# Attention weights turned by VectorE blocks and DMA in place of TensorE, one four-bank score tile, and a stepwise preparation of tokens, in a four-layer transformer kernel

## The chip, the cores and the metric

The program runs on one core of one Trainium2 chip. The metric is the device time in microseconds (us) of one execution. The time before is 2130.87 us, the median of three runs (2130.27 to 2134.04).

## The reference, cut to what matters

The input x has 8 batches of 256 tokens and 512 features, in float32, and stays float32 throughout. Four layers follow one another. Layers 0, 1 and 2 hold an attention, layers 0 and 1 also an MLP, and layer 3 holds eight small experts. The part that the change touches is the attention over one sequence of 256 tokens:

```python
q, k, v = ...                       # layer 0: 8 heads of 64 (one k, one v); layer 1: 16 heads of 32
scores = q @ k.T (+ bias)           # per batch and head: 256 x 256
attn = softmax(scores)
ctx = attn @ v                      # per head: 256 x head size
x = x + ctx_of_all_heads @ Wo.T     # layers 0 and 2; layer 1 adds a bias and multiplies by gamma1
```

Layer 1 divides q and k by their norms per head and has an additive bias of 256 x 256. Layer 2 has a fixed sparse mask. The MLPs go from 512 to 2048 features and back.

## The kernel before, in words

All engines work from one program whose order within each engine is fixed when it is built. A tile scheduler merges the emitted steps into one queue for each engine and places the semaphore waits. Tiles come from pools by tag: a pool "A" of four PSUM banks, a pool "C" of four PSUM banks, a pool "p" of seven SBUF buffers of 512 columns, and so on (`BUFS`, L41). A new tile waits until everything that read the oldest tile of its tag is done.

`attend` (from L611) runs an attention. Its loop has one iteration for each batch b (8) and group g of four heads: two groups in attention0 (layer 0), four in attention1 (layer 1) and attention2 (layer 2). An iteration works on two groups at once:

1. `scored` computes the scores of the new group, four heads in four separate one-bank A tiles (matmul L645), queries on the partitions.
2. `turned` turns the softmax weights of heads 0 and 1 of the group before: four TensorE transposes for each head, against an identity, into a C bank (L702), and one copy back to p, on VectorE (L460) for even heads and on ScalarE (L464) for odd ones.
3. `softmax` of the new group: VectorE takes the row maximum (L659, attention0), or adds the bias and takes the minimum of the negative in one custom operation for each 128 x 256 half (L667, attention1 and 2); ScalarE takes the exponential with a row sum (L672). Reciprocals of the sums (L678) are transposed on VectorE (L682), written to DRAM by a DMA, `spread` (L685), and read back broadcast over partitions by one or two DMAs (L690).
4. `some(quantum)` emits a share of queued work: the projections of the next batch, matmul L585, and the output projection of the batch before.
5. `turned` for heads 2 and 3, then `weighted` (matmul L717, weights times values), then `divided` (VectorE L732 multiplies by the broadcast reciprocals and writes ctxT).
6. after the last group of a batch, its output projection is queued (matmul L585 `C<-wo,ctxT`).

In attention1 and attention2, `prepare` (L500 on) also normalizes the tokens two batches ahead (VectorE L450), transposes them on VectorE in 32 x 32 blocks (L515), writes the tile to DRAM in four DMAs of 128 KB that permute the blocks (`turn`, L520), and `fetch` reads it back (L533, L539), so that tokens become feature-major without TensorE. A scale and a shift then follow on VectorE L472 and ScalarE.

All these DMAs are issued by SyncE (SP), one queue in program order: a wait of one DMA holds those behind it. `project1` prepares q and k of attention1: VectorE adds the bias (L1367), ScalarE squares (L1369), VectorE sums (L1370), GpSimd takes the power -1/2 of 32 columns at once (L1379) and multiplies q and k by it (L1383), TensorE transposes them (L1355).

The MLPs (`mlp`) accumulate four products in the four A banks (L955), which `combined` reads out once for each batch and half (L966 to L974), and compute their up products in C (L908).

Of the kernel before, what the change touches and what calls it, by code (L numbers as in the profile page):

```python
# [32 lines left out]
P = 128  # L34
B, S, D = 8, 256, 512
NT = B * S // P
TB = S // P
# [4 lines left out]
    "n": 4, "hT": 2, "qT": 2, "kT": 2, "v": 2, "ctxT": 6, "p": 7, "qk": 4, "row": 3, "wbig": 8,  # L42
    "A": 4, "C": 4,
# [45 lines left out]
PI_BELOW = 3.1415925  # L89

# [21 lines left out]
def layout(inputs):  # L112
# [10 lines left out]
    def grouped(w):  # L123
# [20 lines left out]
        "bias": np.ascontiguousarray(a["mask_1x1xSxS_ff0"].reshape(S, S)),  # L144
        "vec": np.ascontiguousarray(np.concatenate([vec[k] for k in VEC], 1)),
# [26 lines left out]
class Program:  # L172
# [22 lines left out]
    def bank(self, tag):  # L195
        return self.t([P, 512], tag)

# [25 lines left out]
    def setup(self):  # L223
# [40 lines left out]
        self.n_turn = 0  # L264
        self.half_pi = c([P, 1], "half_pi")
# [156 lines left out]
    def normed(self, xs, eps, rms=False, outs=None):  # L422


        nc = self.nc
        n = len(xs)
        mv = self.t([P, n, 2], f"mv{n}", 2)
        r = self.t([P, n], f"r{n}", 2)
        for i, x in enumerate(xs):
            st = self.t([P, 6], "st", 3)  # L430
            nc.vector.bn_stats(st, x)
            nc.vector.bn_aggr(mv[:, i, :], st)  # L432
        mean, var = mv[:, :, 0], mv[:, :, 1]
        if rms:
            nc.vector.tensor_tensor(r, mean, mean, ALU.mult)
            nc.vector.tensor_tensor(r, r, var, ALU.add)
            nc.gpsimd.tensor_scalar(r, r, eps, None, ALU.add)
        else:
            nc.gpsimd.tensor_scalar(r, var, eps, None, ALU.add)  # L439
        nc.gpsimd.tensor_tensor(r, r, self.neg_half[:, 0:n], ALU.pow)  # L440
        rows = []
        for i, x in enumerate(xs):
            if outs is None:
                y = self.bank("n")
            else:
                y, x = outs[i], x.rearrange("p (k c i) -> p c k i", k=KC, c=4)
            if rms:
                nc.vector.tensor_scalar(y, x, r[:, i : i + 1], None, ALU.mult)
            else:
                nc.vector.tensor_scalar(  # L450
                    y, x, mv[:, i, 0:1], r[:, i : i + 1], ALU.subtract, ALU.mult
                )
            rows.append(y)
        return rows

    def copy(self, i, out, in_, scale=None):

        if i % 2 == 0:
            if scale is None:
                self.nc.vector.tensor_copy(out, in_)  # L460
            else:
                self.nc.vector.tensor_scalar(out, in_, scale, None, ALU.mult)
        elif scale is None:
            self.nc.scalar.copy(out, in_)  # L464
        else:
            self.nc.scalar.activation(out, in_, AF.Copy, scale=scale)

    def modulated(self, i, out, in_, scale, shift):
        if shift is None:
            self.copy(i, out, in_, scale)  # L470
        elif i % 2 == 0:
            self.nc.vector.tensor_scalar(out, in_, scale, shift, ALU.mult, ALU.add)  # L472
        else:
            self.nc.scalar.activation(out, in_, AF.Identity, bias=shift, scale=scale)
# [27 lines left out]
    def prepare(self, name, b, quick=False):  # L502
# [5 lines left out]
        hT = self.t([P, KC * S], "hT")  # L508
        if quick:
            self.ready[name, b] = [hT, self.normed(xs, eps, rms), None, 0]  # L510
            return
        nc = self.nc
        y = hT.rearrange("p (c k t i) -> p c k t i", c=4, k=KC, t=TB)
        self.normed(xs, eps, rms, [y[:, :, :, t, :] for t in range(TB)])
        nc.vector.transpose(hT, hT)  # L515
        kept = self.turns[self.n_turn % 3]
        self.n_turn += 1
        to = kept.rearrange("(c i) (a x) -> a i c x", c=4, a=4)
        for a in range(4):
            nc.sync.dma_start(  # L520
                to[a], hT[32 * a : 32 * a + 32, :].rearrange("p (c x) -> p c x", c=4)
            )
        self.ready[name, b] = [hT, None, kept, 0]
# [17 lines left out]
    def h(self, name, b, quick=False):  # L541


        if (name, b) not in self.ready:
            self.prepare(name, b, quick)
# [12 lines left out]
        def placed(i, c, in_):  # L558
            scale = mod[:, scale_at + c, b : b + 1]
            shift = None if shift_at is None else mod[:, shift_at + c, b : b + 1]  # L560
            self.modulated(i, place[:, c], in_, scale, shift)

        if rows is None:
            for c in range(KC):
                placed(c, c, place[:, c])
# [43 lines left out]
    def attend(self, name, n_groups, hd, project, value, finish, work, key_tiles=(2, 2), biased=None,  # L609
# [27 lines left out]
        def scored(b, g):  # L637
            lhs_rhs = [got[b][0](g, j) for j in range(4)]
            s = [self.bank("A") for _ in range(4)]
            rows = P // hd  # L640
            for j0 in range(0, 4, rows):
                for q in range(TB):
                    for j in range(j0, j0 + rows):
                        lhsT, rhs = lhs_rhs[j]
                        nc.tensor.matmul(  # L645
                            s[j][:, at[q] : at[q] + wide[q]], lhsT(q), rhs(wide[q]),
# [4 lines left out]
        def softmax(s):  # L651
            tot = self.t([P, 4, TB], "tot", 3)
            lows = self.t([P, 4, TB], "low", 3)
            ps = []
            for j in range(4):
                p = self.bank("p")[:, :total]
# [5 lines left out]
                for q in range(TB):  # L662
                    cols = slice(at[q], at[q] + wide[q])
                    src, sign = s[j], 1.0
                    if biased is not None:

                        nc.vector.tensor_tensor_reduce(  # L667
                            p[:, cols], s[j][:, cols], biased[:, cols], -1.0, BIG, ALU.add,
                            ALU.min, low[:, q : q + 1],
                        )  # L670
                        src, sign = p, -1.0
                    nc.scalar.activation(  # L672
                        p[:, cols], src[:, cols], AF.Exp, bias=low[:, q : q + 1], scale=sign,
                        accum_out=tot[:, j, q : q + 1],
                    )
                ps.append(p)
# [18 lines left out]
            return ps, by  # L695

        def turned(j, p):
# [9 lines left out]
            self.copy(j, p, m[:, :total])  # L707

        def weighted(b, g, pT):
            o = self.bank("C")  # L710
            for c in range(nch):
                for k in range(TB):
                    mine = [n for n, (kk, q) in enumerate(pairs) if kk == k]
                    q0 = pairs[mine[0]][1]
                    for i in range(per):
                        j = c * per + i
                        nc.tensor.matmul(  # L717
                            o[i * hd : (i + 1) * hd, c * S + q0 * P : (c + 1) * S],
                            value(got[b][1], g, j, k),
                            pT[j][:, mine[0] * P : (mine[-1] + 1) * P],  # L720
# [3 lines left out]
                        )  # L724
            return o
# [13 lines left out]
        last = None  # L739
        for i in range(B * n_groups + 1):  # L740
# [17 lines left out]
            if last is not None:  # L758
                for j in range(2):
                    turned(j, last[2][0][j])  # L760
            if ahead is not None:
                ahead = (b, g, softmax(ahead[2]))
                if g == 0 and ahead_of:
                    for c in (1, 2) if b == 0 else (b + 2,):
                        if c < B:
                            self.prepare(name, c, quick=c == 1)
                        elif c == B and after is not None:
                            self.prepare(after, 0)
                elif g == 0 and b == B - 1:
                    self.prepare(after, 0)  # L770
            if last is None:
                self.some(3 * quantum)
            elif ahead is None and then is not None:

                b, g, (pT, by) = last
                for j in range(2, 4):
                    turned(j, pT[j])
# [10 lines left out]
            else:  # L788
                self.some(quantum)
                b, g, (pT, by) = last  # L790
                for j in range(2, 4):
                    turned(j, pT[j])
# [58 lines left out]
    def blocked(self, b, hT):  # L851

        if b > 0:
            ts = [self.t([P, S], "ctxT") for _ in range(3)]
        else:

            ts = [t[:, i * S : (i + 1) * S] for t in (self.bank("qk"), self.bank("qk")) for i in range(2)]
            ts = ts[:3]
# [6 lines left out]
        return blocks  # L865

# [8 lines left out]
    def blocked_again(self, b):  # L875
# [3 lines left out]
        ts = [self.t([P, S], "ctxT") for _ in range(3)]  # L879
# [12 lines left out]
    def mlp(self, ups, downs, down_sums, load_ups, load_down, act, h, finish, tail):  # L892
# [29 lines left out]
        def sums(m):  # L922

            g = self.t([P, 4, P], "p")
# [4 lines left out]
            return g  # L929
# [15 lines left out]
        def lower(s, a, sums_of_a):  # L945
            hh, b, p = where(s)
            (y11, t3, y21, y22), (t1, t2, t4) = downs[4 * hh + p][:2]
            if p == 0:
                acc[:] = [self.bank("A") for _ in range(4)]
# [49 lines left out]
        for s in range(n):  # L999
            hh, b, p = where(s)  # L1000
            w = ups[4 * hh + p]
            if p == 0:
# [4 lines left out]
                else:  # L1007
                    ms = [begun(i, x) for i in w]
                    gs = [sums(m) for m in ms]
# [10 lines left out]
            if s > 0:  # L1020
                ms = [begun(i, x) for i in w]
                gs = [sums(m) for m in ms]
# [213 lines left out]
    def layer0_mlp(self):  # L1236
# [52 lines left out]
        def finish(hh, b, ys):  # L1289
# [7 lines left out]
            (self.project1(0, self.got), 22.1),  # L1297
# [36 lines left out]
    def project1(self, b, got):  # L1334
# [28 lines left out]
        for t in range(TB):  # L1363
            ss = self.t([P, 32], "ss", 2)
            q = yield from part(t, 0)
            qs = self.bank("qk")
            nc.vector.tensor_tensor(qs, q, self.q_bias, ALU.add)  # L1367
            sq = self.bank("n")
            nc.scalar.activation(sq, qs, AF.Square)  # L1369
            nc.vector.tensor_reduce(ss[:, 0:16], heads(sq), AX.X, ALU.add)  # L1370
            k_ = yield from part(t, 1)
            ks = self.bank("qk")
            nc.scalar.copy(ks, k_)
            sq = self.bank("n")
            nc.scalar.activation(sq, ks, AF.Square)
            nc.vector.tensor_reduce(ss[:, 16:32], heads(sq), AX.X, ALU.add)

            nc.gpsimd.tensor_scalar(ss, ss, 1e-24, None, ALU.max)
            nc.gpsimd.tensor_tensor(ss, ss, self.neg_half, ALU.pow)  # L1379
            nc.gpsimd.tensor_tensor(ss[:, 0:16], ss[:, 0:16], self.sm, ALU.mult)  # L1380
            for y, at in ((qs, 0), (ks, 16)):
                by = ss[:, at : at + 16].unsqueeze(2).to_broadcast([P, 16, 32])
                nc.gpsimd.tensor_tensor(heads(y), heads(y), by, ALU.mult)  # L1383
            ready.append((qs, ks))
# [26 lines left out]
    def layer1_attention(self):  # L1411
# [3 lines left out]
        self.ups, self.downs = [], []  # L1415

        for i in (0, 1, 2, -1, 3, -2, -3, -4):
            if i >= 0:
                self.layer1_up(i)
            else:  # L1420
                self.layer1_down(-1 - i)
# [22 lines left out]
        def value(v, g, j, k):  # L1444
# [3 lines left out]
            "attention1", 4, 32, self.project1, value, finish, (22.1, 6.8), biased=self.bias,  # L1448
# [8 lines left out]

    def layer1_up(self, i):
        self.ups.append([self.up_load("wfc1T", i)])

    def layer1_down(self, i):
# [3 lines left out]
            ([w[:, c, :] for c in range(4)], [w[:, c, :] for c in range(4, 7)], w[:, 7, :])  # L1465
        )

    def layer1_mlp(self):
# [5 lines left out]
        def act(i, ms, gs):  # L1474
            (m,), (g,) = ms, gs
# [6 lines left out]
            def later():  # L1482
                s = self.t([P, 4, P], "p")
# [78 lines left out]

    def layer2(self):
# [5 lines left out]
            biased=self.mask, extra={7: (self.expert_inputs(0), 1.74)},  # L1569
# [34 lines left out]
    def layer3(self):  # L1604
        nc = self.nc
        n_tiles = 4
        b1, b2 = self.v("b1"), self.v("b2")
# [6 lines left out]
        def hidden(xT, k):  # L1614

            got = [[], []]
            for f in range(2):
                ms = [self.bank("A") for _ in range(2)]
                for j in range(2):
# [4 lines left out]
                    )  # L1624
                for j in range(2):
                    e = 2 * k + j
                    g = self.bank("p")
# [124 lines left out]
```

## Time and profile before

| | before |
|---|---|
| median of three runs | 2130.87 us |
| profiled execution: time | 2125.73 us |
| profiled execution: span | 2123.8 us |
| mean granted TensorE clock | 0.994 |
| DMA moved | 138.18 MB |
| GpSimd busy | 291.3 us (14% of the span) |

The profile is of one execution. The page first gives the busy time of each engine: PE is TensorE's matmuls, PEld its weight loads, DVE VectorE, ACT ScalarE, POOL GpSimd. It then gives the chain of work that ended last, followed back from the last instruction, as shares of the span. After this come the groups of instructions: a line of the kernel, engine, operation, output tile and input tiles, count; busy time, mean duration; and the idle time of the engine before them with what ended it. The mean duration of a matmul is its latency through a pipeline; what matmuls cost in a row is read from pieces of the chain or from the timeline.

The execution falls into stages: attention0 from 50 to 300 us, mlp0 to 885, attention1 to 1295, mlp1 to 1675, attention2 to 1970, and layer 3.

### The profile page before, as it was taken

Reading aid. Unit: us, or ns where it says so; the run is one execution under the profiler, and the core shown is the slowest. Engines: PE = TensorE matmul, PEld = TensorE weight load, DVE = VectorE, ACT = ScalarE, POOL = GpSimd, SP = SyncE. Lnnn points to the kernel's source line nnn. Section 1 sums busy time; section 2 is a strip of 40 time slices with the busy share of each in tenths; the row PEclk is TensorE's granted clock in tenths of the full one; section 3 lists DMA queues with packets and bytes.
Section 4 is the critical chain, followed back from the end, with each engine's and each line's share of the span. In section 5 each row is a group of like instructions: output and inputs, shape, how many; then the busy total and the mean of one; then the engine's idle time right before and its main releaser. Section 6 shows DMA issues by size and latency. Waiting matters only on the chain.

```text
span 2123.8 us, 36492 instructions
## 1 busy us (share of the span) xinstructions
PE 2060.5 (97%) x13282; PEld 1523.8 (72%) x13282; DVE 1349.5 (64%) x4474; ACT 761.1 (36%) x2330; POOL 291.3 (14%) x308
## 2 busy tenths in 40 slices
PE   7999899999999999999999999999999989999999
PEld 4555569999999999855555547999999855555444
DVE  6856665656676555756666665776666777776333
ACT  3424321111111111245555663222222256566644
POOL 1101100000000000144444432000000101010220
PEclk9999999999999999999999999999999999999999
DMA  8320241211230100411112132233211222210001
GB/s 308 115 59 17 91 149 38 73 41 58 76 94 19 36 19 18 100 46 40 37 40 52 44 95 78 85 102 115 94 49 46 76 47 45 57 39 19 11 35 40
DMA packets 172147, 138.18 MB, mean 65 GB/s; under 512 B 77824, under 2 KB 144064, under 8 KB 171968
## 3 DMA queue, kind: packets, MB, share of 16 engines
q1 hardware_dynamic: 171968, 135.86, 21.6%
q8 instruction: 105, 1.72, 0.3%
q14 instruction: 74, 0.61, 0.1%
HBM read 99.87 MB, written 35.95 MB: 64 GB/s over the span
## 4 chain that ended last, share of the span: by engine, by line
PE 81%; DVE 8%; DMA 5%; ACT 2%; POOL 2%; issue 1%; SPq 1%; DVEq 0%; ACTq 0%; POOLq 0%
PE C L908 28%; PE C L585 20%; PE A L955 18%; PE C L702 4%; PE A L645 4%; PE C L717 3%; DMA wqkv<-spread 2%; DVE p L667 1%; PE A L1621 1%; DMA spread<-invT 1%; ACT p L672 1%; PE C L1639 1%; DMA turn<-hT 1%; DMA hT<-turn 1%; DVE p L460 1%
## 5 line engine op out<-in xcount | busy, mean ns | idle before, releaser
L908 PE MATMUL C<-hT,wbig 128*128 128x128 f32 x3072 | 416.3, 275 | 0.0
L908 PEld LDWEIGHTS C<-hT,wbig 128*128 128x128 f32 x3072 | 388.8, 192 | 8.6 <-issue 1.8
L585 PE MATMUL C<-wqkv,hT 128*128 128x512 f32 (+1 forms) x768 | 311.1, 545 | 4.9 <-DVE p L460 3.9
L908 PE MATMUL C<-ctxT,wbig 128*128 128x128 f32 x2160 | 300.0, 275 | 0.0
L672 ACT ACTIVATE p<-p,low 128x256 f32<-128x256 f32 (+1 forms) x512 | 241.9, 475 | 152.7 <-DVE low L667 152.0
L908 PEld LDWEIGHTS C<-ctxT,wbig 128*128 128x128 f32 x2160 | 270.1, 192 | 0.0
L955 PE MATMUL A<-wbig,p 128*128 128x256 f32 x1024 | 242.5, 379 | 0.0
L585 PEld LDWEIGHTS C<-wqkv,hT 128*128 128x128 f32 x768 | 130.9, 191 | 124.7 <-issue 111.2
L667 DVE CUSTOM_DVE_ANT_0 p<-A,row 128x256 f32<-128x256 f32 (+1 forms) x512 | 171.7, 386 | 70.6 <-PE C L717 55.1
L955 PEld LDWEIGHTS A<-wbig,p 128*128 128x128 f32 x1024 | 189.6, 190 | 23.0
L702 PEld LDWEIGHTS C<-ident,p 128*128 128x128 f32 x1152 | 129.3, 142 | 81.3 <-issue 39.6
L925 ACT COPY p<-C 128x128 f32<-128x128 f32 x192 | 51.3, 267 | 371.6 <-PE C L908 370.9
L936 DVE TENSOR_TENSOR p<-p,C 128x256 f32<-128x256 f32 x192 | 79.3, 421 | 162.7 <-PE C L908 160.8
L702 PE MATMUL C<-ident,p 128*128 128x128 f32 x1152 | 165.2, 282 | 15.2 <-DVE p L460 6.8
L585 PE MATMUL C<-wo,ctxT 128*128 128x512 f32 x336 | 158.7, 604 | 5.6 <-DVE ctxT L732 5.5
L439 POOL TENSOR_SCALAR r<-mv 128x2 f32<-128x2 f32 (+1 forms) x28 | 7.2, 256 | 953.0 <-DVE mv L432 953.0
L1276 ACT ACTIVATE p<-C 128x128 f32<-128x128 f32 x64 | 17.8, 278 | 295.9 <-DVE p L936 295.9
L926 DVE TENSOR_TENSOR p<-p,C 128x128 f32<-128x128 f32 x192 | 54.9, 286 | 101.5 <-ACT p L925 99.4
L460 DVE COPY p<-C 128x512 f32<-128x512 f32 (+1 forms) x160 | 100.7, 630 | 23.8 <-PE C L702 23.4
L585 PEld LDWEIGHTS C<-wo,ctxT 128*128 128x128 f32 x336 | 58.7, 190 | 70.5 <-issue 53.8
L672 ACT ACTIVATE p<-A,low 128x256 f32<-128x256 f32 x128 | 59.3, 478 | 120.5 <-DVE low L659 87.9
L464 ACT COPY p<-C 128x512 f32<-128x512 f32 (+1 forms) x160 | 85.5, 535 | 36.0 <-PE C L702 36.0
(226 smaller groups left out, 3064.7 us busy)
## 6 DMA issues: line engine op xcount, KB each, us to landing
turn<-hT SPq DMA_DIRECT2D x120, 128.0 KB
hT<-turn SPq DMA_DIRECT2D x16, 512.0 KB
kept<-hT SPq DMA_DIRECT2D x16, 512.0 KB
hT<-kept SPq DMA_DIRECT2D x16, 512.0 KB
wbig<-spread SPq DMA_DIRECT2D x64, 128.0 KB
hT<-turn SPq DMA_DIRECT2D x112, 64.0 KB
wbig<-in_wada1T SPq DMA_DIRECT2D x6, 1024.0 KB
ctxT<-kept SPq DMA_DIRECT2D x48, 128.0 KB
```

Of the source, the lines that this page charges most:

```text
L460: self.nc.vector.tensor_copy(out, in_)
L464: self.nc.scalar.copy(out, in_)
L585: self.nc.tensor.matmul(out, lhsT(k), rhs(k), start=(k == 0), stop=(k == n - 1))
L645: nc.tensor.matmul(s[j][:, at[q] : at[q] + wide[q]], lhsT(q), rhs(wide[q]), start=True, stop=True,)
L667: nc.vector.tensor_tensor_reduce(p[:, cols], s[j][:, cols], biased[:, cols], -1.0, BIG, ALU.add, ALU.min, low[:, q : q + 1],)
L672: nc.scalar.activation(p[:, cols], src[:, cols], AF.Exp, bias=low[:, q : q + 1], scale=sign, accum_out=tot[:, j, q : q + 1],)
L702: nc.tensor.transpose(m[:, n * P : (n + 1) * P], p[:, at[q] + k * P : at[q] + (k + 1) * P], self.ident,)
L717: nc.tensor.matmul(o[i * hd : (i + 1) * hd, c * S + q0 * P : (c + 1) * S], value(got[b][1], g, j, k), pT[j][:, mine[0] * P : (mine[-1] + 1 ...
L908: nc.tensor.matmul(m[:, c : c + P], w[:, k * P : (k + 1) * P], b[:, k], start=(first and k == 0), stop=(k == steps - 1), skip_group_check= ...
L926: nc.vector.tensor_tensor(g[:, 0, :], g[:, 0, :], m[:, P : 2 * P], ALU.add)
L936: nc.vector.tensor_tensor(g[:, 1:3, :], g[:, 0, :].unsqueeze(1).to_broadcast([P, 2, P]), m[:, 2 * P : 4 * P].rearrange("p (i t) -> p i t", ...
L955: nc.tensor.matmul(acc[at][:, half * S : (half + 1) * S], left, right, start=(p == 0 and half == 0), stop=(p == 3), skip_group_check=True,)
```

## The change: what it does

- In attention0 and attention1, batches 0 to 6, heads 0 and 1 of each group (`in_blocks` returns 2) are no longer turned by TensorE. Their keys are taken in another order by the score matmul (runs of 32 keys, strided), the exponentials are written to one two-bank tile in blocks, VectorE transposes that tile in 32 x 32 blocks, four DMAs write it to DRAM (`put`, the same pattern as for the tokens), and one DMA reads it back into the same tile. `weighted` reads it strided. Heads 2 and 3, attention2 and the last batch keep the TensorE path.
- A group's scores lie in one A tile of four banks, of which there is one (`"A": 1`); mlp and layer 3 use the same tile.
- The p pool has four two-bank buffers in place of seven one-bank ones, ctxT four buffers in place of six; the MLP's working tiles are regrouped to match, and `three` takes its extra blocks in turn from qk and ctxT.
- `prepare` is a generator: in attention1 and 2 it is emitted in up to three steps, one for each iteration, in place of all at once.
- The scale and shift of the fetched tokens (`placed`), and the matmuls that read turned weights, are kept in program order (`keep_in_program_order`), so the scheduler doesn't move other instructions of their engine past them.
- `project1` handles q and k separately (GpSimd power on 16 columns each, L1379 before), squares k straight from PSUM, and the start of layer 1 loads a copy of the bias in block order.

The diff, cut to its core:

```diff
-    "n": 4, "hT": 2, "qT": 2, "kT": 2, "v": 2, "ctxT": 6, "p": 7, "qk": 4, "row": 3, "wbig": 8,
-    "A": 4, "C": 4,
+    "n": 4, "hT": 2, "qT": 2, "kT": 2, "v": 2, "ctxT": 4, "p": 4, "qk": 4, "row": 3, "wbig": 8,
+    "A": 1, "C": 4,
...
+    def four(self):
+        t = self.t([P, 4, 512], "A")
+        return [t[:, i, :] for i in range(4)]
...
+    def in_blocks(self, name, b):
+        return 2 if name != "attention2" and b < B - 1 else 0
+
+    def put(self, kept, tile):
         to = kept.rearrange("(c i) (a x) -> a i c x", c=4, a=4)
         for a in range(4):
-            nc.sync.dma_start(
-                to[a], hT[32 * a : 32 * a + 32, :].rearrange("p (c x) -> p c x", c=4)
+            self.nc.sync.dma_start(
+                to[a], tile[32 * a : 32 * a + 32, :].rearrange("p (c x) -> p c x", c=4)
             )
...
         if rows is None:
             for c in range(KC):
-                placed(c, c, place[:, c])
+                self.tc.keep_in_program_order(placed(c, c, place[:, c]))
...
-            s = [self.bank("A") for _ in range(4)]
+            s = self.four()
...
+                        keys = rhs(wide[q])
+                        if j < self.in_blocks(name, b):
+                            keys = keys.rearrange("p (k c i) -> p c k i", c=4, i=32)
...
+                if j == 3 and n_blocks:
+                    nc.vector.transpose(blocks, blocks)
+                    kept = self.flips[self.n_flip % 4][:, : 2 * total]
+                    self.n_flip += 1
+                    self.put(kept, blocks)
+                    nc.sync.dma_start(blocks, kept)
             inv = self.inv[self.n_spread % 2]
...
-                for j in range(2):
-                    turned(j, last[2][0][j])
+                weights = last[2][0][1]
+                for j, p in enumerate(weights[: len(weights) // 2]):
+                    turned(j + len(weights) % 4 // 2, p)
...
-                            self.prepare(name, c, quick=c == 1)
+                            steps.append(self.prepare(name, c, quick=c == 1))
...
+                for step in steps:
+                    for _ in step:
+                        if b > 0 and ahead_of:
+                            break
+                    else:
+                        done.append(step)
...
-            nc.gpsimd.tensor_tensor(ss, ss, self.neg_half, ALU.pow)
...
+                nc.gpsimd.tensor_tensor(r, r, self.neg_half[:, 0:16], ALU.pow)
```

In the built program, the plain heads 2 and 3 are transposed in two places of an iteration (head 2 after the scores, head 3 later). The instruction queues of the two programs, which can be compared before any run, are used in the prediction.

## The prediction, on record before the run

> **What bounds the kernel now.** I read the page's busy times and chain first, then the busy times by stage, then the chain inside one batch of each attention. The page:
>
> ```profile
> PE 2060.5 (97%) x13282; PEld 1523.8 (72%) x13282; DVE 1349.5 (64%) x4474; ACT 761.1 (36%) x2330; POOL 291.3 (14%) x308
> ...
> PE 81%; DVE 8%; DMA 5%; ACT 2%; POOL 2%; issue 1%; SPq 1%; DVEq 0%; ACTq 0%; POOLq 0%
> ...
> L702 PE MATMUL C<-ident,p 128*128 128x128 f32 x1152 | 165.2, 282 | 15.2 <-DVE p L460 6.8
> ```
>
> TensorE is busy 97% of the span, so the whole program has 63 us without it. The 1152 turns at L702 are real TensorE work. By stage (columns: window, its length, PE, PEld, DVE, ACT, POOL busy, clock, DMA share, GB/s):
>
> ```profile
> 50.00:300.00 250.00, 233.04 (x1362) 139.50 (x1361) 166.17 (x464) 89.92 (x298) 35.13 (x61) 0.99 0.25 76
> 300.00:885.00 585.00, 585.00 (x4404) 560.29 (x4403) 367.21 (x1194) 91.40 (x281) 6.53 (x14) 1.00 0.18 55
> 885.00:1295.00 410.00, 397.50 (x2260) 214.50 (x2259) 259.77 (x879) 222.73 (x679) 172.01 (x126) 0.99 0.21 54
> ```
>
> The MLP has no gap at all. Attention0 has 17 us of gaps and attention1 12.5 us. So TensorE work removed from an attention counts in full, unless it turns into a wait there. What ends last inside a batch decides that. In attention0 the chain from 179 to 212 us has:
>
> ```profile
> 199.60 1.97 DMA spread<-invT
> ...
> 202.18 8.14 DMA wqkv<-spread
> 210.32 0.02 issue
> 210.34 0.44 DVE ctxT L732
> 210.78 0.04 issue
> 210.82 1.55 PE C L585 x3
> ```
>
> This batch runs from 179.49 to 210.82, 31.3 us with 29.9 of PE; its end is a DMA, the broadcast of the reciprocals. In attention1 a batch lasts 47.6 us (1113.65 to 1161.28) with 46.5 of PE: PE sets it.
>
> **Removed work.** Two heads of four transposes go in 2 × 7 groups of attention0 and 4 × 7 of attention1, 42 groups × 8 = 336 turns. The row's 282 ns is latency; in the chain eight in a row take 0.87 to 1.02 us ("1106.06 0.87 PE C L702 x8", "1112.63 1.02"), so one takes 0.116. That is 0.93 a group, 39 us in all: 13 in attention0 (1.86 a batch), 26 in attention1 (3.7 a batch). Per group one VectorE copy (0.63, L460) and one ScalarE copy (0.54, L464) go too, and one VectorE block transpose comes (1.2, the 128x1024 L515). VectorE gains 0.6 us a group; it is under 65% busy in both attentions, so I cost it at nothing unless it sits ahead of a copy that PE awaits, then 0.6.
>
> **Strided operands.** No row shows these. By the nearest row they are free: L908's hT operand is already read in 32-element runs, and twelve 128-column pieces take 1.50 us in the timeline (1424.15), less a latency of 0.275 0.111 each, while L585's dense 512-column ones take 7.03 for sixteen (1161.12), 0.107 for 128 columns. Taking that 4% on the 16 affected matmuls a group (about 2 us) as the upper end gives 0.08 a group, 3 us in all; the lower end is zero[...]. I take zero.
>
> **The DMA turn.** Four puts and one get are the same pattern as the tokens' L520 and L533/L539. The trace's chain shows 3.08 us from the last issue to landing (1067.42, 1251.96), issues of 0.3 to 0.6 each, and 3.94 and 4.61 us for gets. A flip lasts 1.2 + 1.8 + 3.1 + 4 ≈ 10 us. The Trainium skill speaks against it: "VectorE: DVE Perf Modes", section "The three transpose paths", says that a plain DMA whose strides do the transpose is 19 times slower than the crossbar DMA, and its rules section sends a 128x128 transpose to TensorE. As an estimate, 19 times the 3.94 us get would be 75 us a group against a group time of 12 to 15, some 2500 us over 42 groups. The row decides: elements are turned on VectorE, the DMA moves runs of 1 KB (128 KB puts in 128 runs), and they land in 3.1. By the row 7 us stay, not 75. In attention1 the weights are needed one group (12 us) after their exponentials start; by the two orders the tightest group has 2.4 us to spare. I cost it at nothing there; without the cover, up to 2 us a group.
>
> **Attention0: the queue.** The get waits on SP for the puts to land, and behind it in SP's order stand the broadcast reads that set the batch's end. Counting from the last group's scores (187.41 before), spread was issued at +12.2 and the reads landed at +22.9. One thing comes earlier: ScalarE's seventh exponential waited for a free p tile:
>
> ```profile
> 197.57 0.48 ACT L672 ACTIVATE p<-A,low 128x256 f32<-128x256 f32 x1 [2.98 <-PE C L717]
> ```
>
> With two-bank p tiles this 3 us wait goes: exponentials end by +6, VectorE's transpose by +7, the puts land by +11.5, the get is issued at +11.8 and holds the DMA engines to about +14.7 (2.9, my estimate from its 3.94 less the 1 us of a landing), and the reads, 7 to 8 us, land at +22.1. Then 0.4 for ctxT. That is 0.7 a batch gained of the 1.86 removed, 5 us in all. The bounds: 13 if the reads are not late, and a loss of 10 (1.5 a batch) if they wait for the get to land (4 rather than 2.9).
>
> **Attention1: one score tile.** The four-bank A tile means that scores of a group wait for all eight reads (L667) of the group before. Mostly they are 12 us apart. But in the order of the changed program, at each batch start, scores g0 are followed by one piece of projection (0.86 us) and then five of the eight score matmul pairs of g1. In before's trace:
>
> ```profile
> 1159.11 1.15 PE L645 MATMUL A<-kT,qT 32*128 32x256 f32 x16
> 1160.19 1.09 PE L702 MATMUL C<-ident,p 128*128 128x128 f32 x8
> 1161.12 7.03 PE L585 MATMUL C<-wqkv,hT 128*128 128x512 f32 x16
> ```
>
> The next scores came at 1170.99, 11.9 later, and the eight reads ran at 0.345 each behind bn_stats, from 1161.66 to 1164.42. Put into the new order, PE is free at +1.9 from the first scores and the reads end at +4: 2 us idle, with all projections queued behind the waiting score matmul. After these scores the next projection piece needs the fetched tokens scaled by ScalarE. That step is pinned in program order behind eight exponentials (0.49 each, 3.9 in all), so it ends at +6.2, where PE wants it at +4.6: 1.6 more. Against that, before's 1.1 idle a batch partly goes. The sum for a batch: 47.6 − 3.7 + 2.0 + 1.6 − 1.1 − about 0.7 of overlap between the waits and copies ≈ 45.7, −1.9 a batch, 13 in all. Bounds: −26 (no new wait) and +7 (the two waits at 3 and 2.5 with a late copy after).
>
> **Attention1's start.** PE waited there for GpSimd's power: "906.00 5.46 POOL ss L1379" for 32 columns, while 2 columns take 0.71. Linear between them, 16 columns take about 2.9 (an estimate), so q's chain begins earlier: −3 us (0 to −5). Two of 16 columns cost GpSimd 0.4 more than one of 32; it is 42% busy there, which hides it.
>
> **Attention2** keeps its turns and gets only the new waits: the scale pinned behind exponentials and the single A tile. Its order is less squeezed; I take +0.8 a batch (0 to 1.5), +6. **MLPs, layer 3:** the single A tile makes the first accumulation of a batch wait for the last read of `combined` (L973). In mlp1, the tighter one, that read ends at 1424.66 and the next accumulation began at 1425.94: 1.3 us of cover, 15 times; nothing, or +5 if VectorE falls 1.6 behind. The steps of `prepare` move token work (two statistics, two L450, the 1.2 us transpose, four puts) from one iteration to three; its puts land behind flips on SP. Their tokens are needed a batch later, 47 us: nothing, or the 3 us of a late put once a batch if that cover went.
>
> **Sum.** −5 − 13 − 3 + 6 + 3 (start-up of attention0, whose first flips queue behind 1 MB weight loads; 0 to 4) = −12. The profiled execution, 2125.7 with 2123.8 of span and 1.9 around it, becomes 2114. It is 5.1 us below the median; the same step puts the median at 2130.9 − 12 ≈ 2119.
>
> **Rivals.** (a) *The work simply goes*: −39 − 3 and no new wait of weight, 2089 to 2096. For it: PE sets attention1, and flips are covered. Against: the order at each batch start shows both waits. Chance 0.2. (b) *No change*: attention0's end is the DMA chain anyway, and attention1's waits at the batch start eat the 3.7 saved: −5 + 0 − 3 + 6 + 3 ≈ 0, 2127 to 2135. Chance 0.12. (c) *Slower*: the single score tile. Its place is the head of each batch in attention1 and attention2, its price the wait for eight reads (up to 2.8 of reads plus what VectorE does first) and for the pinned ScalarE step (up to 3.9). From 3.7 a batch on, it eats what attention1 saves; at 5, with +2 in attention2 and +1 in attention0, the sum is 7 × 1.3 + 8 × 2 + 7 × 1 − 3 = +29, half of it +15: 2140 to 2160. For it: PE's queue is in order, and 7 of 8 batches have it. Against: VectorE is idle 37% of attention1. Chance 0.31. (d) The forecast, 2105 to 2127, 0.37. A change that doesn't do what it says is excluded by the program: PE's queue has 336 transposes less.
>
> **Chances and range.** About 0.2% (4.3 us) is what a measurement can tell from no change. Faster: (a), (d): 0.57; within: 0.12; slower: 0.31. The range 2093 to 2150 leaves out the best of (a) and the worst of (c), about 0.1 each; the forecast's own range is 2105 to 2127.
>
> **What would show it.** L702 falls from 1152 to 816. A row "PE A scores <- DVE low" with 2 us a batch, and one "PE projection <- ACT hT", show the attention1 waits; a batch of 45.7 instead of 47.6. In attention0, reads still end the chain, a batch of 30.6. ScalarE's wait for p at L672 (26.6 us in the list of waits) goes. The prediction is wrong if attention1's batches are near 44 (no wait) or at 47 and above, or if `weighted` waits for the get.

## The result and the profile after

The changed kernel takes 2185.5 us, the median of four runs, beside 2130.6 before: 1.0259 times as long, 95% interval 1.0240 to 1.0277. The prediction was 2119, with a range up to 2150: wrong in sign. The profiled execution has a span of 2182.7 us, 58.9 more than before's 2123.8.

The page of the changed kernel, with the three lines that answer to those shown of before:

```profile
PE 2069.9 (95%) x12946; PEld 1489.5 (68%) x12946; DVE 1346.1 (62%) x4432; ACT 747.7 (34%) x2326; POOL 305.0 (14%) x340
...
PE 81%; DVE 7%; ACT 5%; DMA 3%; POOL 2%; issue 1%; SPq 0%; ACTq 0%; DVEq 0%; POOLq 0%
...
L757 PE MATMUL C<-ident,p 128*128 128x128 f32 x816 | 120.3, 280 | 11.4 <-ACT p L722 8.8
```

The 336 turns are gone (13282 matmul records became 12946), and yet TensorE is busy 9.4 us longer. That line already says that the loss isn't only a new wait: the remaining work also runs more slowly.

I cut both executions at the same events: first and last up matmul of each MLP (L908 before, L988 changed), first up matmul of layer 3. An up matmul is one of the product that widens the features.

| stage, us | predicted change | before | changed | measured change |
|---|---|---|---|---|
| start to the end of mlp0 | −2 | 888.0 | 889.7 | +1.7 |
| attention1 | −16 | 398.7 | 413.0 | +14.3 |
| mlp1 | 0 | 404.6 | 405.3 | +0.7 |
| attention2 | +6 | 277.2 | 293.1 | +15.9 |
| layer 3 | 0 | 155.3 | 181.6 | +26.3 |

**Attention1.** The list of TensorE's waits in the whole changed kernel (total, times, longest) has the two that were predicted; the scores at L680 wait for the reads of the score tile (L718), the projection at L616 for ScalarE's half of the tokens' scale (L494). Of these, 15.8 us in 7 waits and 5.2 in 6 are attention1's:

```profile
PE A L680 <- DVE low L718: 25.2, 14, 4.4
...
PE C L616 <- ACT hT L494: 7.2, 7, 2.0
```

One batch start in TensorE's timeline (start, duration, line, pieces, idle time before it):

```profile
1069.77 1.15 PE L680 MATMUL A<-kT,qT 32*128 32x256 f32 x16
1070.85 1.13 PE L616 MATMUL C<-wqkv,hT 128*128 128x512 f32 x2
1074.01 1.15 PE L680 MATMUL A<-kT,qT 32*128 32x256 f32 x10 [2.03 <-DVE low L718]
1076.07 8.22 PE L616 MATMUL C<-wqkv,hT 128*128 128x512 f32 x12 [0.91 <-ACT hT L494]
1084.22 1.07 PE L782 MATMUL C<-p,v 128*32 128x256 f32 x16
```

The waits are 2.0 and 0.9 us; 2.0 and 1.6 were predicted. What wasn't predicted stands in the fourth line: twelve projection pieces take 8.15 us from start to start, where they cost 0.43 each, 5.2 in all. The stage rows (window, length, busy time of PE, PEld, DVE, ACT, POOL, clock, DMA share, GB/s) say why:

```profile
1076.07:1081.50 5.43, 5.43 (x7) 2.34 (x8) 0.00 (x0) 0.43 (x1) 0.00 (x0) 0.50 0.87 197
...
1084.30:1119.64 35.34, 35.34 (x200) 17.25 (x201) 23.59 (x78) 20.84 (x65) 22.77 (x19) 1.00 0.41 101
```

Behind the first wait the granted clock falls to 0.50 for 6.8 us, then it is 1.00 for the rest of the batch. A batch became 49.9 us (1069.77 to 1119.64): 47.6 before, −4.0 of turns (L757 is busy 4.83 in this batch, L702 was busy 8.86), +1.9 of waits (2.9 for 1.1), +3.0 of half clock, and +1.4 because score and weighting matmuls are split into shorter groups (L680 is busy 5.30, L645 was busy 4.51; L782 4.90, L717 4.28). The sum is 49.9. The steady batches last 48.8 to 52.2 us; in every other one the half clock lasts only 3.4 us, and the twelve pieces cost 1.6 to 1.8 more, not 3.

The Trainium skill, "TensorE: Matmul & The Clock Gate", section "Why this matters for your kernels", warns of idle gaps over some 3 us between matmuls, after which the clock halves. Here no single gap in the steady batches is longer than 2.3 us, and the clock fell all the same. The traces show when. Their clock records change only on a grid of 3.41 us, and this batch's fall comes after the first wait and before the second:

```profile
1071.51:1074.92 3.41, 1.38 (x12) 0.69 (x10) 3.41 (x15) 3.41 (x14) 0.00 (x0) 1.00 0.37 120
1074.92:1081.74 6.82, 5.91 (x8) 2.53 (x8) 0.66 (x4) 1.58 (x6) 0.00 (x0) 0.50 0.76 178
```

The step ahead of the fall holds 2.0 us without a matmul, in one gap; ahead of the five other falls in attention1's batches it holds 2.0 to 2.3, in one gap or two. In the 13 traces of this case 73 steps at full clock held 1.95 us or more without a matmul, and the clock was 0.50 in the next step each time; of the 7546 with less than 0.9, it was so after five. Between these bounds both happen.

**Layer 3.** The table's cut is not clean here: 2.7 of the 26.3 us are work of attention2, of which more now follows the first up matmul. Counted from the end of attention2's last projection, layer 3 takes 145.2 us before and 168.8 changed, 23.6 more:

```profile
1978.58:2123.80 145.22, 140.98 (x559) 62.18 (x558) 51.10 (x95) 70.46 (x116) 19.91 (x20) 1.00 0.08 30
```

```profile
2013.91:2182.70 168.79, 162.32 (x559) 62.12 (x558) 51.76 (x95) 71.82 (x117) 19.87 (x20) 1.00 0.07 25
```

The clock is full and the work is the same, 559 matmul records, but TensorE is busy 21 us longer. The down matmuls, which bring the features back, take most of it: L1639 was busy 29.9 us, L1737 is busy 47.3; the up matmuls went from 32.8 to 39.5. Its timeline before:

```profile
1978.58 4.18 PE L1621 MATMUL A<-qk,wbig 64*128 64x512 f32 x14
1982.69 3.65 PE L1639 MATMUL C<-p,wbig 128*64 128x512 f32 x16
```

and changed:

```profile
2015.81 1.07 PE L1737 MATMUL C<-p,wbig 128*64 128x512 f32 x2 [0.78 <-ACT p L1726]
2016.82 1.13 PE L1718 MATMUL A<-qk,wbig 64*128 64x512 f32 x4
2017.88 1.98 PE L1737 MATMUL C<-p,wbig 128*64 128x512 f32 x4
2019.79 1.13 PE L1718 MATMUL A<-qk,wbig 64*128 64x512 f32 x4
```

A down matmul uses 64 of the array's columns (128*64), and is two records. Eight in a row took 3.58 us, 0.45 each: the two of a pair ran side by side, their records start 0.007 us apart. Between up matmuls each record starts alone, one half of a pair at a time, and two matmuls take 1.9, 0.95 each. In these stretches half of the array stood unused.

**The start.** The first batches of attention0 wait for the turn's DMAs and, at L1228, for ctxT, whose broadcast reads are queued behind them:

```profile
55.61 1.95 PE L782 MATMUL C<-p,kT 128*64 128x256 f32 x16 [1.61 <-DMA p<-flip]
...
67.03 0.45 PE L1228 MATMUL C<-ident,kr 128*128 128x128 f32 x1 [8.34 <-DVE ctxT L799]
```

From 30 to 80 us TensorE is busy 31.3 us at a clock of 0.80; before it was 44.3 at 0.93. Later, an attention0 batch is 29.75 us (177.26 to 207.01) where it was 31.0, cut at the same scores (169.78 to 200.81). By its first up matmul mlp0 starts 2.6 us earlier (288.8 for 291.4), but it takes 600.9 for 596.6; why it does stays open.

### The profile page after: what moved, and what is told of

The parts are those of the page before. It is cut to its first block, busy times and chain, and to the rows that moved or that the text cites. A ratio compares the mean times of both kernels' runs of the same rounds, so it can differ in the third digit from the quotient of the medians.

```text
span 2182.7 us, 36203 instructions
## 1 busy us (share of the span) xinstructions
PE 2069.9 (95%) x12946; PEld 1489.5 (68%) x12946; DVE 1346.1 (62%) x4432; ACT 747.7 (34%) x2326; POOL 305.0 (14%) x340
## 4 chain that ended last, share of the span: by engine, by line
PE 81%; DVE 7%; ACT 5%; DMA 3%; POOL 2%; issue 1%; SPq 0%; ACTq 0%; DVEq 0%; POOLq 0%
PE C L988 27%; PE C L616 20%; PE A L1037 17%; ACT p L722 4%; PE A L680 4%; PE C L782 3%; PE C L757 3%; PE C L1737 2%; PE A L1718 2%; DVE p L718 1%; DVE low L702 1%; DMA wqkv<-spread 1%; DVE p L727 1%; PE C L320 1%; POOL ss L1464 1%
## 5 line engine op out<-in xcount | busy, mean ns | idle before, releaser
L988 PE MATMUL C<-hT,wbig 128*128 128x128 f32 x3072 | 419.1, 275 | 0.0
L988 PEld LDWEIGHTS C<-hT,wbig 128*128 128x128 f32 x3072 | 390.3, 192 | 9.1 <-issue 2.2
L616 PE MATMUL C<-wqkv,hT 128*128 128x512 f32 (+1 forms) x768 | 329.5, 567 | 5.6 <-ACT hT L494 5.2
L616 PEld LDWEIGHTS C<-wqkv,hT 128*128 128x128 f32 x768 | 134.6, 198 | 127.9 <-issue 112.0
L616 PE MATMUL C<-wo,ctxT 128*128 128x512 f32 x336 | 161.2, 612 | 7.0 <-DVE ctxT L799 7.0
L988 PE MATMUL C<-qk,wbig 128*128 128x128 f32 x1152 | 160.0, 275 | 0.0
L988 PE MATMUL C<-ctxT,wbig 128*128 128x128 f32 x1152 | 160.0, 275 | 0.0
L718 DVE CUSTOM_DVE_ANT_0 p<-A,row 128x256 f32<-128x256 f32 (+1 forms) x400 | 127.5, 377 | 36.6 <-PE A L680 30.8
L988 PEld LDWEIGHTS C<-ctxT,wbig 128*128 128x128 f32 x1152 | 144.3, 192 | 0.2
L988 PEld LDWEIGHTS C<-qk,wbig 128*128 128x128 f32 x1152 | 144.2, 192 | 0.1
L757 PEld LDWEIGHTS C<-ident,p 128*128 128x128 f32 x816 | 92.1, 141 | 66.6 <-issue 37.9
L757 PE MATMUL C<-ident,p 128*128 128x128 f32 x816 | 120.3, 280 | 11.4 <-ACT p L722 8.8
L680 PE MATMUL A<-kT,qT 32*128 32x256 f32 (+2 forms) x896 | 84.2, 407 | 29.7 <-DVE low L718 22.8
L616 PEld LDWEIGHTS C<-wo,ctxT 128*128 128x128 f32 x336 | 59.9, 192 | 75.6 <-issue 55.4
L680 PEld LDWEIGHTS A<-kT,qT 32*128 32x128 f32 (+1 forms) x896 | 51.6, 194 | 77.0 <-issue 53.7
```

Of the source, the lines that this page charges most:

```text
L616: self.nc.tensor.matmul(out, lhsT(k), rhs(k), start=(k == 0), stop=(k == n - 1))
L680: nc.tensor.matmul(s[j][:, at[q] : at[q] + wide[q]], lhsT(q), keys, start=True, stop=True,)
L718: nc.vector.tensor_tensor_reduce(out, src, by, -1.0, BIG, ALU.add, ALU.min, low[:, q : q + 1])
L757: nc.tensor.transpose(m[:, n * P : (n + 1) * P], p[:, at[q] + k * P : at[q] + (k + 1) * P], self.ident,)
L988: nc.tensor.matmul(m[:, c : c + P], w[:, k * P : (k + 1) * P], b[:, k], start=(first and k == 0), stop=(k == steps - 1), skip_group_check= ...
```

## The experiments

Two suspects stand for the loss: the one four-bank tile, and the pin, that is `keep_in_program_order` on the tokens' scale. Each was undone alone, both together, and each was put alone into the kernel before (of the pin, half). Ratios are to the kernel before on the same chip, with 95% intervals.

**Four tiles again.**

```diff
-    "A": 1
+    "A": 4
     def four(self):
-        t = self.t([P, 4, 512], "A")
-        return [t[:, i, :] for i in range(4)]
+        return [self.bank("A") for _ in range(4)]
...
-                ms = [banks[(2 * k + f) % 2 * 2 + j] for j in range(2)]
+                ms = [self.bank("A") for _ in range(2)]
```

> The changed kernel with four one-bank score tiles again (in the attentions, the MLPs and layer 3), all else as changed. Theory (the one tile and the pinned step share the loss): layer 3 returns to its chunk of 35.9 us from 39.9 and the end of the program gets 26 us back, attention2 some 6; attention1 stays near 49 us a batch, because its order and the pinned step stay; 2185 becomes 2145 to 2158. Rival A (the one tile is the whole cause): attention1 returns to about 44 to 46 a batch too, 2095 to 2115. Rival B (the DMA turn itself costs, by its waits or its traffic): 2175 to 2185.

Measured: 2154.5 us, ratio 1.0122 (1.0107 to 1.0137), as the theory said. Layer 3 falls from 181.6 to 159.6. Attention1 stays at 411.7 and attention2 at 295.3: there the one tile isn't what costs, and the 6 us that the theory put in attention2 did not come. In attention1 the scores' waits do go (1.4 us for 15.8), but the score matmuls now come apart and are busy 57.4 us for 44.9. Rival A falls.

**No pin.**

```diff
-                self.tc.keep_in_program_order(placed(c, c, place[:, c]))
+                placed(c, c, place[:, c])
```

> The changed kernel without the pin on the scale and shift of the fetched tokens (the matmuls on turned weights stay pinned). Theory: at each batch start of attention1 the waits of 2.0 and 1.0 us go, and with them the stretch at half clock after them (2 to 3 us a batch); attention1's batch falls from 49.9 to 44 to 46, the granted clock of that stage from 0.95 to 0.99 or more; layer 3 stays slow; 2185 becomes 2145 to 2160. Rival A (one tile): within 6 us of 2185. Rival B: the same, within 6 us.

Measured: 2136.1 us, ratio 1.0038 (1.0020 to 1.0056), lower than expected. Attention1 takes 379.5 in place of 413.0, at a clock of 0.98, and attention2 277.2, as before the change. A batch start now:

```profile
1082.82 1.15 PE L680 MATMUL A<-kT,qT 32*128 32x256 f32 x16
1083.90 0.66 PE L757 MATMUL C<-ident,p 128*128 128x128 f32 x4
1084.39 1.88 PE L616 MATMUL C<-wqkv,hT 128*128 128x512 f32 x4
...
1093.30 1.15 PE L680 MATMUL A<-kT,qT 32*128 32x256 f32 x16
```

The second scores are 10.5 us behind the first, not 4.2, with the one tile still there: it was the pin that brought them forward. The likely reason, which no run shows by itself: while ScalarE's step stood behind eight exponentials, the scheduler had no projection to place, so the next scores came first and met the tile's readers. A batch is 43.45 us (1082.82 to 1126.27), 4.2 less than before the change.

**Both undone.**

> The changed kernel with four one-bank score tiles and without the pin, together. Theory: both losses go and the saved TensorE work shows: 2100 to 2118, below before. Rival A: 2095 to 2115 as in the run with four tiles alone. Rival B (the DMA turn costs what it saves): 2130 to 2150.

Measured: 2116.0 us, ratio 0.9941 (0.9927 to 0.9956). With these two undone the kernel is faster than before, so they turn the gain into a loss. They are not the only ones: attention2 takes 283.9 here, 6.7 more than before and more than with the one tile kept (277.2). That stays open.

**One tile alone, in the kernel before.**

> The kernel before with one four-bank score tile, all else as before. Theory: layer 3 loses its 26 us as in the changed kernel, attention1 loses about nothing (its scores stay 10 us apart in this order), attention2 0 to 8: 2130 becomes 2152 to 2165. Rival A: attention1 loses too, 2180 or more. Rival B: within 5 us of before.

Measured: 2151.1 us, ratio 1.0107 (1.0090 to 1.0124), just under the theory's range. Layer 3 takes 177.7 (+22.4), attention2 280.9 (+3.7), attention1 390.6, which is 8.1 less than before, a gain that no theory expected.

**The pin alone, in the kernel before** (ScalarE's half; with VectorE's half pinned as well this kernel deadlocks, so the whole pin has no time of its own here).

```diff
+                ins = placed(c, c, place[:, c])
+                if c % 2 == 1:
+                    self.tc.keep_in_program_order(ins)
```

> The kernel before with ScalarE's half of the tokens' scale and shift pinned in program order (VectorE's half not), all else as before: the pin alone. Theory: ScalarE reaches that step only after the eight exponentials of the batch's first group, TensorE's projections come later, and attention1 and attention2 get longer together by 15 to 45 us: 2142 to 2172. Rival (the pin hurts only together with the one score tile or the turn's order): 2122 to 2134.

Measured: 2159.8 us, ratio 1.0163 (1.0139 to 1.0187). Attention1 takes 419.8 (+21.1), attention2 291.1 (+13.9), layer 3 155.4. The pin hurts without the tile and without the turn. Its form differs here: the second group's scores are torn apart,

```profile
1126.06 0.63 PE L716 MATMUL C<-p,v 128*32 128x256 f32 x6 [1.45 <-DVE p L460]
1126.62 0.69 PE L644 MATMUL A<-kT,qT 32*128 32x256 f32 x2
1127.36 1.05 PE L716 MATMUL C<-p,v 128*32 128x256 f32 x10
...
1130.26 0.69 PE L644 MATMUL A<-kT,qT 32*128 32x256 f32 x2
```

so that single score matmuls with 32 of the array's rows run without their neighbours, 0.6 to 0.7 us each, where eight together take 1.08. In a batch of 51.0 (1109.69 to 1160.66) L644 is busy 5.95 for 4.51 before, L716 4.90 for 4.28, TensorE idles 2.5 for 1.1, and the clock is 1.00: here the loss comes without any half clock.

**Layer 3's order alone.** Pins on the up and down matmuls of layer 3, on top of the version without the other pin.

> The changed kernel without the pin on the tokens' scale, still with one four-bank tile, but with layer 3's two kinds of matmul (up and down of the experts) kept in the order they are emitted in, so that the two matmuls of a pair stand together again. Theory (in layer 3 the one tile costs only through the order it brings about, which parts the pairs that use half the array each): layer 3 from its first matmul falls from 181.9 us to 155 to 162, 2136 becomes 2110 to 2118. Rival (the one tile costs by waits for its readers): layer 3 stays at 175 or more, 2130 to 2140.

Measured: 2136.9 us, ratio 1.0032 (1.0024 to 1.0041): no gain, as the rival said. The pairs stand together, as the theory wanted, but now:

```profile
1967.71 1.13 PE L1718 MATMUL A<-qk,wbig 64*128 64x512 f32 x4 [1.36 <-ACT p L1727]
1970.26 2.08 PE L1718 MATMUL A<-qk,wbig 64*128 64x512 f32 x4 [1.42 <-ACT p L1727]
1974.03 2.08 PE L1718 MATMUL A<-qk,wbig 64*128 64x512 f32 x4 [1.69 <-ACT p L1727]
```

Each pair of up matmuls waits for the GELUs that read the pair before, though they are in other banks of the tile: 15.5 us in 12 waits. So with one tile each pair waits for the readers of the last, whichever bank they read; the scheduler had filled that wait with down matmuls, at the price of parting their pairs. The half clock shows here too (2.08 for four records, 1.13 at full clock); its mean over layer 3 is 0.95. Counted from the end of attention2's last projection (1965.3 here), layer 3 takes 171.9 us, 168.8 in the changed kernel and 145.2 before: either way it loses 24 to 27.

**The clock.** Five extra matmuls after the first scores of each batch, into a bank that nobody reads, in the changed kernel.

```diff
+            if name == "attention1" and g == 0 and b > 0:
+                m = self.bank("C")
+                lhsT, rhs = lhs_rhs[0]
+                for n in range(5):
+                    nc.tensor.matmul(m[:, 0:256], lhsT(n % 2), rhs(256), start=True, stop=True)
```

> The changed kernel with five extra matmuls after the first scores of each batch of attention1, into a bank that nobody reads (work added, 2.1 us of TensorE a batch), so that TensorE is busy through the wait for the score tile. Theory (idle time in front of it halves the clock for the next 4 to 7 us): with the wait filled, the clock stays up in attention1's batches, and adding 2.1 us of work makes a batch shorter: 49.9 becomes 46 to 47.5, 2185 becomes 2160 to 2172. Rival (the clock falls for another reason, such as the load of the projections that follow): the granted clock stays at 0.93 to 0.97 there and a batch at 49.5 to 51, 2183 to 2192.

Measured: 2182.3 us, ratio 1.0263 (1.0239 to 1.0287): the same as the changed kernel, where 13 to 25 less were expected. Attention1 takes 406.6, 6.4 less, with 7 × 2.2 us of work more in it. Between the starts of the added work, five batches last 50.6, 48.2, 47.1, 50.2 and 47.1 us. Those at 47.1 keep the full clock, as expected; so does the one at 50.6, whose length has another cause. The one at 50.2 doesn't:

```profile
1111.41 1.15 PE L681 MATMUL A<-kT,qT 32*128 32x256 f32 x16 [0.78 <-DVE kT L483]
1112.38 3.00 PE L689 MATMUL C<-kT,qT 32*128 32x256 f32 x10
1115.31 1.97 PE L765 MATMUL C<-ident,p 128*128 128x128 f32 x8
```

Here the clock halved for 6.8 us from 1113.9 on, after a step with 0.78 us of idle time; it is one of the five steps named above. The added work uses 32 of 128 rows; in all five, matmuls on the whole array filled less than 0.7 us of the step. But 163 other steps as thin kept the full clock, so that such work counts as half idle isn't shown. What is shown: behind its start, attention1 is at half clock for 31 us in six falls in the changed kernel, and for 14 us in three with the wait filled. With the count of steps above, long idle time is what a fall follows; what brings one about after a short idle time stays open.

**What the turn is worth.**

> The version with four one-bank tiles and without the pin (2116), with no head turned by DMA: all four heads of every group by TensorE again. It prices the turn itself. If the turn is worth what it removes less the new waits, attention1 gets about 18 us longer (380.9 to 396 to 404) and attention0 5 (286 to 289 to 295), 2116 becomes 2130 to 2142. If the turn is worth nothing and the gain of that version came from the other parts: 2111 to 2121.

Measured: 2163.2 us, ratio 1.0152 (1.0137 to 1.0167), 47 more than with the turn and far above either forecast. Attention1 takes 420.0 for 380.9, which is 39 and not the 26 of TensorE's turns; the rest is TensorE waiting for VectorE's copies of turned weights ("PE C L615 <- DVE p L482: 13.9, 10"), which the turn also takes away. So the turn is worth 47 inside this version, not against the kernel before: without turn, one tile and pin, what is left of the change still costs 1.5%, and 21 us in attention1 (420.0 for 398.7). Which part costs that stays open; the p pool of four two-bank buffers and the shorter ctxT pool were not tried alone.

> The version at 2116, with the turn in attention1 alone. Theory: attention0's steady batches lose the 1.5 us each that the turn gave (7 to 9 in all) and its start gains 5 to 9: 2113 to 2121. If the turn is worth nothing in attention0's steady batches because the DMA sets their end: 2106 to 2112.

Measured: 2126.1 us, ratio 0.9985 (0.9977 to 0.9992). Without the turn in attention0, mlp0 ends at 897.9 in place of 886.3. That is above both forecasts. So the turn pays in attention0 too, some 10 us, and the DMA does not set the end of its batches.

> The version at 2116, with no turn in attention0's first batch. Theory (the first batch's turn queues behind the 1 MB weight loads, leaves TensorE idle for 8 to 10 us, and a stretch at half clock follows): the stretch from 40 to 80 us returns to the kernel before, attention0 ends 5 to 9 us earlier, 2107 to 2112. Rival (the wait there has another cause): 2114 to 2118.

Measured: 2113.6 us, ratio 0.9922 (0.9908 to 0.9937), between theory and rival, and only 2.4 us from the version at 2116: the intervals of the two ratios overlap. Attention0 ends 5.7 us earlier (280.5 for 286.2), mlp0 only 2.9; from 30 to 80 us TensorE is busy 43.9 again (36.6 in the version at 2116).

> The version with four one-bank tiles, no pin and no turn in attention0's first batch (2113.6), with the tokens prepared at once as before, in place of in three steps. If the steps are worth nothing, as predicted: 2110 to 2118. If they are worth their own: 2119 to 2130.

Measured: 2111.4 us, ratio 0.9926 (0.9908 to 0.9944): the steps are worth nothing. This version and the one above are the fastest here, 0.7 to 0.8% below before.

## Why the prediction was wrong, step by step

- **Removed work, 39 us: right, and worth more.** In attention1 a batch without the pin is 4.2 us shorter than before, where 3.7 were counted; its turns went from 8.86 to 4.83. (VectorE was busy 166.17 of 250.00 us in attention0, 66% and not under 65%; nothing hung on it.)
- **Strided operands, the DMA turn's cover: right.** A group of sixteen weighting records takes 1.07 us strided (1084.22), as it did dense (1120.45 before). `weighted` waited for a get twice, 3.7 us in all; that was named as a sign of being wrong, but it is no part of the loss in attention1. The rule that was weighed against the row (19 times slower) didn't apply; the row did. The Trainium skill, "VectorE: DVE Perf Modes", section "The three transpose paths", has the 19 for a large innermost stride at the destination, and against the time of the crossbar DMA; the estimate multiplied the time of a plain get.
- **Attention0: the queue: too pessimistic in the batch, too kind at the start.** 29.75 a batch for the predicted 30.6. The reads no longer end the chain, which there runs through reductions and exponentials, and ScalarE's wait for a p tile is gone, as predicted. The start was put at +3; without the turn in the first batch attention0 ends 5.7 us earlier.
- **Attention1's start, −3: the size held, the gain did not come.** GpSimd's power of 16 columns takes 2.92 us, 2.9 were estimated. But the first scores come 33.1 us after mlp0's last up matmul, 30.1 before; at their head they wait for the MLP to read out the one tile:

```profile
922.76 1.15 PE L680 MATMUL A<-kT,qT 32*128 32x256 f32 x16 [3.06 <-DVE n L1055]
```

- **"Attention1: one score tile": waits right, cause wrong, sum wrong.** Predicted 3.6 us of waits a batch, found 2.4 to 3.3. But undoing the tile gives 1.3 us of the stage and undoing the pin 33.5. The failed step is the sum for a batch: it priced a wait by its length. It left out the 1.6 to 3.1 us of half clock behind the wait and the 1.4 of split groups, and took 0.7 off for an overlap that isn't there: 45.7 predicted, 49.9 measured. A batch of 47 and above was named as a sign of being wrong.
- **Attention2, +6: mis-sized.** +15.9, and undoing the pin alone takes it away (277.2 without). A steady batch is 35.6 us for 33.8 without the pin: 0.7 of it idle time (2.25 for 1.58), 0.5 and 0.6 in scores and weighting (L680 busy 4.71 for 4.22, L782 4.66 for 4.04), whose groups are split in two.
- **"MLPs, layer 3": the gravest failure.** The paragraph worked out mlp1's cover, which held (+0.7), and gave layer 3 nothing and no reason, though the same four-bank tile was put there. It is the largest loss, 26.3 us by the table and 23.6 by the cleaner cut: the one tile lets each pair of up matmuls start only behind the readers of the last, and the order that fills this wait parts the pairs.
- **Rival (c), slower:** the sign was right, its place wrong. It looked for the tile in attention1 and attention2; the tile costs in layer 3, and in the attentions it is the pin, which the rival named second. 2185.5 lies 25 us above its 2160.

## What to carry to other kernels

A tile of several banks is one thing to whatever tracks its readers: before merging tiles, list every stage that cycles through their banks. A pin in program order moves more than the pinned step; compare the order of the engine that waits for it. Price an idle gap of TensorE by the half-clocked work that follows, and matmuls that use part of the array by whether their neighbours stay next to them.

## What the runs showed of the hardware

The granted clock fell to 0.50 after each of 73 steps of 3.41 us that held 1.95 us or more without a matmul, though no gap in attention1's steady batches was longer than 2.3 us. A matmul on 64 columns costs 0.45 us beside its pair and 0.95 alone. A lone score matmul on 32 rows costs 0.6 to 0.7, and eight together 1.08.
